# A three-layer graph network with attention: attention in seven stages instead of five, and layer 0's side work spread over more groups

## The chip, the cores and the metric

The kernel runs on one core of a Trainium2 chip. Its time is the device time of one execution in microseconds (us), and less is better. The core has five engines that work side by side, each through its own queue of instructions in a fixed order: TensorE (PE; its weight loads are shown apart as PEld), VectorE (DVE), ScalarE (ACT), GpSimd (POOL) and SyncE (SP), which here only issues transfers. They wait for each other by semaphores. Transfers (DMA) between the main memory and the core's memory are issued by SP, ACT and POOL.

## The reference, cut to what matters

There are 12500 nodes of 256 values and 200000 edges, sorted by their target `dst`. Three layers average over the edges; then one attention step follows, with four heads of 16 values.

```python
# layers 0, 1, 2 (relu after the first two)
agg  = segment_sum(x[src], dst, N)
x    = x @ W_self + (agg * inv_deg[:, None]) @ W_neigh + b
...
# attention
ZU   = einsum('nd,kdr->knr', Z, U)
zs, zd = ZU[:, src, :], ZU[:, dst, :]
logits = (zs * zd).sum(-1) / 4
alpha  = softmax of logits over the edges of one target
agg    = segment_sum(alpha[..., None] * zs, dst)
ssa    = einsum('k,knr,kdr->nd', w, agg, U)
Z_half = 0.5 * Z + 0.5 * ssa
grad   = Z_half + 0.5 * (Z_half - Z_half @ Dmat.T @ Dmat) @ Dmat
x = layernorm(Z + relu(grad - 0.05))
```

## The kernel before, in words

**Groups.** Because edges are sorted by target, 1792 successive edges (14 tiles of 128) touch a range of at most 128 targets. There are 112 such groups. The sum over the edges of a group is a product with a one-hot matrix (`oh`, L453: edge against target), 14 tiles added up in one PSUM bank. What a group's first target still had from the group before it is added by one more product (`carry`, L460). The sources' rows come by indirect transfers that POOL issues, one for each tile of 128 edges, so 14 a group (`gather`, L119).

**Sage layers.** Layers 1 and 2 do this for the targets of lower number (76 groups), and layer 0 for 94 groups. The other targets are handled densely: first a table of counts (how many edges lead from a source to a target) is formed by products of two one-hot matrices (`form`, L603 to L638: DVE makes `oa` and `ob` at L622, PE multiplies at L630, ACT turns the result to bytes at L633), and then the table multiplies all source rows (`sweeps`, L673 to L755, the product at L740). For that, x is split into two parts that add up to it (`split_x`, L499 to L529), and the position where each target's edges end is counted (`row_ends`, L532 to L541; `count_ends`, L554). In layer 0 all of this runs beside the groups. How much of it goes with which group is planned by hand: `due(l, g)` says how many steps of the sweeps are to be done by group g, `built(g)` how many steps of forming, and the loop at L893 to L917 hands them out between the stages of the groups, with ten splits of x a group. GA, G1 and GB are the groups where these plans bend.

**Attention.** `fast_attention` (L929 to L1029) is a generator for each group. A `yield` ends a stage, and the loop at L1019 to L1028 takes each living group on by one stage in a round. In the first stage, group g loads `zn`, `zb`, `zT` and the row for `ohT` by SP, starts 14 gathers of `zs` by POOL, makes `oh` (DVE) and `ohT` (ACT, L958 and L959), splits `zn` in two (`z2`), multiplies (`pD`, L970: the target's values for each edge, in two halves of seven tiles), and forms from it the logits (DVE `zz` L977, `lg` L980), their exponentials (ACT L983) and a copy of these in PSUM (ACT L985), the weighted rows (DVE `wf` L986, the last to read `zs` and `pD`), and their two parts (`w`, ACT L989 and DVE L990). The second stage sums over the edges (`pA`, L993 and L460). The third reads the sums (ACT `part` L1000, DVE `acc` L1002), divides (`den`, `ag`, L384 to L387) and transposes (PE `pT` L1006). The fourth makes the gradient step (ACT `agT` L394, PE `pO` L376 and L377). The fifth ends it (ACT `g` L401, DVE L402 and the layernorm L332 to L337) and stores by SP.

**What sets the order.** A tile has as many buffers as its `bufs` says; the next user of a buffer waits for the last reader of the one before it. `zs` has six, and `pD` two, one for each half.[...] On PE the order is that of the source, since `in_order` chains every group of products to the one before it. On DVE, ACT, POOL and SP the order is fixed when the program is built, from the order of the source and from what is expected to be ready. It isn't always that of the source: the trace shows L401 of an older group between L983 and L985 of a newer one.

Of the kernel before, what the change touches and what calls it, by code (L numbers as in the profile page):

```python
# [9 lines left out]
F32 = mybir.dt.float32  # L10
F32R = mybir.dt.float32r
# [11 lines left out]
P = 128  # L23
NB = 125
TE = 125
GT = 14
# [11 lines left out]
ZB = 2  # L38
# [9 lines left out]
def tile_gnn_resnorm(  # L48
# [16 lines left out]
    K, _, R = u.shape  # L65
    KR = K * R
    DC = D // P
    NBLK = N // NB
    NG = -(-E // GE)
    L = len(w_self)  # L70
    AW = KR + K
    N0 = N - ND * P
    NQ = -(-N // P)
# [3 lines left out]
    NU = ND // SG0  # L77
    U0 = NU - NDL[0] // SG0
    parts = [*range(U0, NU), *range(U0)]

    def part_at(u):

        return max(0, (E * (N0 + u * SG0 * P) // N - SLACK) // GE - GD)
# [4 lines left out]
    needs = [part_groups[u] - part_at(U0) if u >= U0 else NM - part_at(U0) + part_groups[u] for u in range(NU)]  # L88
# [78 lines left out]
    rel = const.tile([P, NG, GT], F32, name="rel")  # L167
# [18 lines left out]
    with tc.tile_pool(name="prep", bufs=1) as prep, \  # L186
# [42 lines left out]
        for nd, c in cuts.items():  # L229
            a, m = c.GS, c.NGS - c.GS  # L230
# [28 lines left out]
        for i, c in enumerate(cuts.values()):  # L259
            a = NM + 2 + 2 * i  # L260
# [176 lines left out]
    def after(first, then):  # L437

        tc.add_manual_dep(then.ins, first.ins.name, AFTER, reason="the order of the work")
# [4 lines left out]
    def group_consts(cps, n=P):  # L444

        c = cps.tile([P, n], F32, name="gconst")
        nc.vector.tensor_copy(c, iota[:, :n])
        return c

    def onehot(wk, nodes, r, dt=F32, name="oh", op=OP.is_equal, bufs=2):  # L450

        oh = wk.tile([P, GT, P], dt, name=name, bufs=bufs)
        nc.vector.tensor_tensor(oh, r.unsqueeze(2).to_broadcast([P, GT, P]),  # L453
                                nodes.unsqueeze(1).to_broadcast([P, GT, P]), op=op)
        return oh
# [6 lines left out]
    def fast_sage():  # L462
        with ExitStack() as fx:
            wp = fx.enter_context(tc.tile_pool(name="sage_w", bufs=1))
            wk = fx.enter_context(tc.tile_pool(name="sage", bufs=2))
# [12 lines left out]
            nodes = group_consts(cps)  # L478
# [73 lines left out]
            counted = [0]  # L552

            def count_ends(pool, n):  # L554
                for g in ends_of[counted[0]:n]:
                    row_ends(pool, g)
                    counted[0] += 1
# [199 lines left out]

            PER = SG0 * P // NC
            BUILDS = 3 + NU * PER
            GA, G1, GB = 3, 7, 62  # L760

            def due(l, g):
                sg, ahead = (SG, 0) if l else (SG0, G1)
                n, end = NDL[l] // sg * NQ, cuts[NDL[l]].NGS - LAG - sg // 2
                if g >= end:
                    return n + (2, 2, 4)[l] * min(sg, 2 * (g + 1 - end))
                if l:
                    return n * (g + 1) // end

                return max(0, n * (g + 1 - G1) // (GB - G1) // 2 if g < GB else n - n * (end - g - 1) // (end - GB) // 2)  # L770

            def built(g):
                if g < GA:
                    return g + 1
                if g < G1:
                    return 3 + PER * (g + 1 - GA) // (G1 - GA)
                return min(BUILDS, 3 + PER + (BUILDS - PER - 3) * (g + 1 - G1) // (GB - G1))

            turn = 0
            for l in range(L):  # L780
# [6 lines left out]
                with ExitStack() as lx:  # L787
# [5 lines left out]
                    if l == 0:  # L793
                        tk = lx.enter_context(tc.tile_pool(name="tabs", bufs=1))
# [4 lines left out]
                    def group(g):  # L799
# [10 lines left out]
                        oh = onehot(wk, nodes, srel, F32R if halved else F32)  # L810
# [58 lines left out]
                            nc.scalar.activation(part, pa[:, D:], AF.Copy)  # L869
                            nc.vector.tensor_add(before[:, :D], part, pa[:, :D])  # L870
                        sums = before[:, :D] if l else pa[:, :D]
                        if l == 0 and g == 0:
                            count_ends(tk, needs[U0])
                        mean = wk.tile([P, D], F32, name="mean", bufs=3)
                        nc.scalar.activation(mean, sums, AF.Copy, scale=inv[:, g:g + 1])  # L875
                        if not l:
# [15 lines left out]
                    live, stages = [], (2, 2, 4)[l]  # L892
                    for g in range(cut.NGS + stages // 2):  # L893
                        units, turns = [], [s for s in live for _ in range(2)]
                        if g < cut.NGS:
                            live.append(group(g))
                            todo, more = due(l, g) - done, built(g) - formed if l == 0 else 0
                            done, formed = done + todo, formed + more
                            n = max(todo, more)
                            for i in range(n):  # L900
                                units += [forming] * ((i + 1) * more // n - i * more // n)
                                units += [steps_] * ((i + 1) * todo // n - i * todo // n)
                            next(live[-1])
                        if l == 0 and g < cut.NGS:

                            soon = min(NU, 1 + max(0, built(g + 1) - 3 + PER - 1) // PER)
                            count_ends(tk, max(counted[0] + 1, max(needs[u] for u in parts[:soon])))
                            for _ in range(10):
                                next(xsplit, None)
                        n = len(turns) + 1  # L910
                        for i in range(n):
                            for u in units[len(units) * i // n:len(units) * (i + 1) // n]:
                                next(u, None)
                            if i < len(turns):
                                next(turns[i])
                        if g >= stages // 2:
                            live.pop(0)  # L917
# [11 lines left out]
    def fast_attention():  # L929
        loads[0] = None  # L930
        H = GT // 2
        with tc.tile_pool(name="att", bufs=2) as wk, \
                tc.tile_pool(name="att_c", bufs=1, space=PSUM) as cps, \
                tc.tile_pool(name="att_ps", bufs=1, space=PSUM) as ps:
            nodes = group_consts(cps)
            order, sums = [None], [None]

            def in_order(first, last):
                if order[0] is not None:
                    after(order[0], first)  # L940
                order[0] = last

            def group(g):

                zb = wk.tile([P, D], F32, name="zb", bufs=8)
                zT = wk.tile([P, DC, P], F32, name="zT", bufs=6)
                zn = wk.tile([P, KR], F32, name="zn", bufs=3)
                load_rows([(zn, zu_d), (zb, z_d), (zT, zt_d)], g)

# [4 lines left out]
                zs = wk.tile([P, GT, KR], F32, name="zs", bufs=6)  # L954
                for j in range(GT):
                    gather(zs[:, j], zu_d, srcI[:, g, j:j + 1])
                oh = onehot(wk, nodes, rel[:, g], F32R, bufs=3)
                nc.scalar.activation(ohT.rearrange("p j e -> p (j e)"), rT, AF.Abs, bias=npidx)  # L958
                nc.scalar.activation(ohT.rearrange("p j e -> p (j e)"), rT, AF.Relu, scale=-1.0, bias=1.0)  # L959

# [2 lines left out]
                nc.scalar.activation(z2[:, :, 0], zk, AF.Copy)  # L963
                nc.vector.tensor_tensor(z2[:, :, 1], zk, z2.bitcast(F32)[:, :, 0], op=OP.subtract)

                w = wk.tile([P, GT, 2 * AW], F32R, name="w", bufs=3)
                for a in (0, H):

                    pd = ps.tile([P, (H + 1) * 2 * KR], F32, name="pD", bufs=2)
                    mm = [nc.tensor.matmul(pd[:, j * 2 * KR:(j + 1) * 2 * KR], ohT[:, a + j],  # L970
                                           z2.rearrange("p k i r -> p (k i r)"), start=True, stop=True)
                          for j in range(H)]
                    in_order(mm[0], mm[-1])

                    zg = zs[:, a:a + H].rearrange("p t (k r) -> p (t k) r", r=R)
                    zz = wk.tile([P, H * K, 2, R], F32, name="zz")
                    nc.vector.tensor_mul(zz, zg.unsqueeze(2).to_broadcast([P, H * K, 2, R]),  # L977
                                         pd[:, :H * 2 * KR].rearrange("p (m i r) -> p m i r", i=2, r=R))
                    lg = wk.tile([P, H, K], F32, name="lg")
                    nc.vector.reduce_sum(lg.rearrange("p t k -> p (t k)"), zz.rearrange("p m i r -> p m (i r)"),  # L980
                                         axis=AX.X)
                    wf = wk.tile([P, H, AW], F32, name="wf")
                    nc.scalar.activation(wf[:, :, KR:], lg, AF.Exp, scale=0.25)  # L983
                    pe = pd[:, H * 2 * KR:H * (2 * KR + K)].rearrange("p (t k) -> p t k", k=K)
                    nc.scalar.activation(pe, wf[:, :, KR:], AF.Copy)  # L985
                    nc.vector.tensor_mul(wf[:, :, :KR].rearrange("p t (k r) -> p t k r", r=R),  # L986
                                         zs[:, a:a + H].rearrange("p t (k r) -> p t k r", r=R),
                                         pe.unsqueeze(3).to_broadcast([P, H, K, R]))
                    nc.scalar.activation(w[:, a:a + H, :AW], wf, AF.Copy)  # L989
                    nc.vector.tensor_tensor(w[:, a:a + H, AW:], wf, w.bitcast(F32)[:, a:a + H, :AW], op=OP.subtract)  # L990
                yield
                pa = ps.tile([P, 2 * AW], F32, name="pA")
# [22 lines left out]
                yield  # L1015

            live = []  # L1019
            for g in range(NG + 4):  # L1020
                if g < NG:
                    live.append(group(g))
                    next(live[-1])
                old = live[:-1] if g < NG else live
                for s in old:
                    next(s)
                if g >= 4:
                    live.pop(0)  # L1028
            assert not live  # L1029

# [203 lines left out]
```

## Time and profile before

| | |
|---|---|
| median of 3 runs | 8820.85 us (8773.32 to 8844.72) |
| the profiled execution | 8849.94 us, its span 8848.1 us |
| granted clock of PE, mean | 0.744 |
| PE busy | 5720.5 us (65%) |
| PE weight loads | 4442.3 us (50%) |
| DVE busy | 3939.4 us (45%) |
| ACT busy | 3599.7 us (41%) |
| POOL busy | 4894.3 us (55%) |

The profile names a group of instructions by its line and the tile that it writes and reads (`pD<-z,ohT`), with a count (x14). "Idle before" is the time that the engine did nothing just ahead of an instruction, and behind the arrow stands what ended it; "issue" and "remote" are waits whose end the profile can't name. The ends of PE's products are modelled. PE's sequence of stages can be told by the lines: layer 0 has L844, layers 1 and 2 have L838, attention has L970.

The chain of work that ended last gives every line a small share:

```profile
PE 9%; issue 7%; another core or an unknown queue 6%; DVE 5%; POOL 2%; ACT 2%; DMA 1%; DVEq 0%; ACTq 0%
```

Its shares add up to 32% of the span, so it covers attention and little before it, and some two fifths of it carry no name of an engine's work (issue, and a queue that the profile can't name).

### The profile page before, as it was taken

How to read it: one execution, taken by the hardware profiler on the slowest of the kernel's cores; microseconds unless marked ns; L12 is line 12 of the kernel's file. 1: busy time of each engine (PE TensorE's matmuls, PEld its weight loads, DVE VectorE, ACT ScalarE, POOL GpSimd, SP SyncE). 2: the span in 40 equal slices, each digit the busy share in tenths (PEclk: the TensorE clock that was granted, in tenths of full speed). 3: DMA queues.
4: the chain of work that ended last, by engine and by line, in shares of the span. 5: the costliest groups of instructions: out<-in, count | busy, mean ns of one | idle time of the engine just before them, and what ended most of it. 6: DMA issues, size and time to landing. Idle time of an engine off the chain costs nothing. (4 is left out here: it accounts for less than half of the span.)

```text
span 8848.1 us, 86603 instructions
## 1 busy us (share of the span) xinstructions
PE 5720.5 (65%) x23308; PEld 4442.3 (50%) x23308; DVE 3939.4 (45%) x10013; ACT 3599.7 (41%) x6544; POOL 4894.3 (55%) x5038
## 2 busy tenths in 40 slices
PE   4666676777757777777677787877524444444445
PEld 2344454555546656666456665666423333333334
DVE  4544444433433333334434444444524544544455
ACT  2433443434434444444344443444324444444444
POOL 4444555555546655555555554555366666666653
PEclk7787888878778888888788898898755555555555
DMA  6644555566646666666466665666322322322232
GB/s 186 218 157 157 161 177 166 176 202 207 204 153 195 201 195 191 205 202 198 156 182 189 181 197 171 189 186 185 106 62 82 86 84 84 87 85 84 83 86 67
DMA packets 878809, 1367.35 MB, mean 155 GB/s; under 512 B 191091, under 2 KB 533131, under 8 KB 874208
## 3 DMA queue, kind: packets, MB, share of 16 engines
q1 hardware_dynamic: 629744, 802.71, 28.3%
q0 software_dynamic: 216000, 504.16, 20.4%
q10 hardware_dynamic: 32559, 54.81, 1.8%
q8 instruction: 187, 3.06, 0.1%
q14 instruction: 319, 2.61, 0.1%
HBM read 1150.87 MB, written 210.33 MB: 154 GB/s over the span
## 5 line engine op out<-in xcount | busy, mean ns | idle before, releaser
L119 POOL DMA_INDIRECT xg<-h_d,srcI x2128 | 2111.5, 992 | 1698.0 <-issue 479.3
L740 PE MATMUL px<-c,hz 128*128 128x512 f32 x7840 | 2500.3, 457 | 378.6 <-issue 254.7
L740 PEld LDWEIGHTS px<-c,hz 128*128 128x128 f32 x7840 | 1616.5, 212 | 1103.5 <-issue 649.7
L119 POOL DMA_INDIRECT zs<-zu_d,srcI x1568 | 1490.4, 951 | 993.8 <-issue 440.1
L119 POOL DMA_INDIRECT xg<-in_x_dram,srcI x1274 | 1230.9, 966 | 1150.1 <-PE pA L844 571.3
L734 ACT ACTIVATE c<-c 128x1024 fp32r<-128x1024 uint8 (+1 forms) x1176 | 1067.1, 911 | 1477.0 <-remote 648.4
L453 DVE TENSOR_TENSOR oh<-rel,gconst 128x1792 fp32r<-128x1792 f32 (+1 forms) x358 | 722.7, 2019 | 1539.2 <-remote 861.0
L1006 PE MATMUL pT<-ident,ag 128*64 128x128 f32 x112 | 47.1, 421 | 1330.0 <-DVE ag L387 1207.2
L833 DVE TENSOR_TENSOR hl<-xg,hl 128x256 fp32r<-128x256 f32 x2128 | 769.8, 416 | 116.5 <-ACT mean L875 47.6
L831 ACT ACTIVATE hl<-xg 128x512 fp32r<-128x512 f32 x1064 | 613.1, 620 | 500.8 <-remote 135.6
L633 ACT ACTIVATE win<-pc 128x392 uint8<-128x392 f32 x1024 | 478.4, 499 | 693.8 <-remote 311.6
L1006 PEld LDWEIGHTS pT<-ident,ag 128*64 128x64 f32 x112 | 14.4, 128 | 1413.3 <-DVE ag L387 1284.8
L630 PE MATMUL pc<-ob,oa 128*128 128x392 bf16 x1024 | 375.1, 393 | 469.7 <-ACT win L633 287.2
L838 PE MATMUL pA<-hl,oh 128*128 128x512 f32 x2128 | 554.3, 408 | 73.6 <-issue 63.1
L838 PEld LDWEIGHTS pA<-hl,oh 128*128 128x128 f32 x2128 | 410.6, 194 | 179.6 <-issue 71.9
L844 PE MATMUL pA<-xg,oh 128*128 128x258 f32 x1764 | 449.5, 395 | 3.2 <-DVE oh L453 3.0
L352 PE MATMUL pO<-ws,hT 128*128 128x256 f32 x984 | 312.9, 448 | 189.6 <-DVE hT L363 103.9
L986 DVE TENSOR_TENSOR wf<-zs,pD 128x448 f32<-128x448 f32 x224 | 129.9, 617 | 619.5 <-issue 444.5
L970 PE MATMUL pD<-z,ohT 128*128 128x128 f32 x1568 | 362.0, 418 | 59.7 <-issue 24.0
L844 PEld LDWEIGHTS pA<-xg,oh 128*128 128x128 f32 x1764 | 346.8, 199 | 89.6 <-issue 33.5
L977 DVE TENSOR_TENSOR zz<-zs,pD 128x896 f32<-128x896 f32 x224 | 242.6, 1083 | 325.8 <-remote 148.2
L970 PEld LDWEIGHTS pD<-z,ohT 128*128 128x128 f32 x1568 | 348.0, 333 | 60.6 <-issue 41.3
(251 smaller groups left out, 8354.5 us busy)
## 6 DMA issues: line engine op xcount, KB each, us to landing
hz<-hs_d SPq DMA_DIRECT2D x588, 512.0 KB
c<-cnt_d SPq DMA_DIRECT2D x112, 896.0 KB
ohT<-rel_d SPq DMA_DIRECT2D x112, 896.0 KB
hs_d<-hs SPq DMA_DIRECT2D x218, 256.0 KB
cnt_d<-win ACTq DMA_DIRECT2D x32, 1568.0 KB
xg<-h_d,srcI POOLq DMA_INDIRECT x2128
c<-cnt_d SPq DMA_DIRECT2D x56, 448.0 KB
zs<-zu_d,srcI POOLq DMA_INDIRECT x1568
```

What stands on the lines that cost most here:

```text
L119: return nc.gpsimd.indirect_dma_start(out=dst_ap, out_offset=None, in_=table, in_offset=bass.IndirectOffsetOnAxis(ap=idx, axis=0))
L352: mm = [nc.tensor.matmul(po, hT[:, i], wts[i // DC][:, i % DC], start=i == 0, stop=i == 2 * DC - 1) for i in range(2 * DC)]
L453: nc.vector.tensor_tensor(oh, r.unsqueeze(2).to_broadcast([P, GT, P]), nodes.unsqueeze(1).to_broadcast([P, GT, P]), op=op)
L630: mm = nc.tensor.matmul(pc.rearrange("p b d -> p (b d)"), oa[:, c], ob[:, c], start=True, stop=True)
L633: nc.scalar.activation(win[:, :, d:d + NC], pc, AF.Copy)
L734: nc.scalar.activation(c32.rearrange("p (k d) -> p k d", d=P), c8[:, :, b % CB], AF.Copy)
L740: made.append(nc.tensor.matmul(px[f][i], hz[:, b % ZB, a:a + P].bitcast(F32R), c32[:, i * 512:(i + 1) * 512], start=b == 0 and part == 0, ...
L831: nc.scalar.activation(hi[:, j:j + 2, :W], xg[:, j:j + 2, :W], AF.Copy)
L833: nc.vector.tensor_tensor(lo[:, j, :D], xg[:, j, :D], hf[:, j, :D], op=OP.subtract)
L838: mm.append(nc.tensor.matmul(pa, oh[:, j], hl[:, j].rearrange("p i d -> p (i d)"), start=first, stop=stop))
L844: mm.append(nc.tensor.matmul(pa[:, :W], oh[:, j], xg[:, j, :W], start=first, stop=stop))
L970: mm = [nc.tensor.matmul(pd[:, j * 2 * KR:(j + 1) * 2 * KR], ohT[:, a + j], z2.rearrange("p k i r -> p (k i r)"), start=True, stop=True) f ...
```

## The change

In attention a group now goes through seven stages. The loads and the gathers are a stage by themselves. The second stage makes `oh`, `ohT`, `z2` and both halves of `pD`. The third reads `pD` and makes the weights: first the logits, exponentials and their copy for both halves, then the weighted rows and first parts of both, then the second parts of both. The other four stages stay as they were. A round first begins the newest group and then takes on the others from the oldest to the youngest. That was so before as well, but what the newest group began with was everything up to `w`, and now it is its loads and gathers alone. `zT` has seven buffers for six, and `oh` four for three.

In layer 0 the plan is flatter at the start. The first seven counts of ends no longer stand together in group 0; three go with group 0, four with group 1. Forming begins in group 2 for group 0, and its first 128 products are spread over groups 5 to 13, where they stood in groups 3 to 6. x is split in five steps a group for ten. The sweeps begin with group 14 for 7, and two fifths of them are done by group 62, where it was half.

```diff
-            GA, G1, GB = 3, 7, 62
+            GA, G1, GB = 5, 14, 62
...
-                return max(0, n * (g + 1 - G1) // (GB - G1) // 2 if g < GB else n - n * (end - g - 1) // (end - GB) // 2)
+                n1 = n * 2 // 5
+                return max(0, n1 * (g + 1 - G1) // (GB - G1) if g < GB else n - (n - n1) * (end - g - 1) // (end - GB))
 
             def built(g):
                 if g < GA:
-                    return g + 1
+                    return max(0, g + 4 - GA)
...
-                        if l == 0 and g == 0:
-                            count_ends(tk, needs[U0])
...
-                            soon = min(NU, 1 + max(0, built(g + 1) - 3 + PER - 1) // PER)
-                            count_ends(tk, max(counted[0] + 1, max(needs[u] for u in parts[:soon])))
-                            for _ in range(10):
+                            soon = min(NU, 1 + max(0, built(g + 1) - 3 + PER - 1) // PER) if built(g + 1) else 0
+                            count_ends(tk, max(counted[0] + (1 if soon else needs[U0] // 2),
+                                               max((needs[u] for u in parts[:soon]), default=0)))
+                            for _ in range(-(-NQ // ZB // (G1 - 2))):
                                 next(xsplit, None)
...
-                zT = wk.tile([P, DC, P], F32, name="zT", bufs=6)
+                zT = wk.tile([P, DC, P], F32, name="zT", bufs=7)
...
-                oh = onehot(wk, nodes, rel[:, g], F32R, bufs=3)
+                yield
+                oh = onehot(wk, nodes, rel[:, g], F32R, bufs=4)
...
-                w = wk.tile([P, GT, 2 * AW], F32R, name="w", bufs=3)
+                halves = []
                 for a in (0, H):
-
                     pd = ps.tile([P, (H + 1) * 2 * KR], F32, name="pD", bufs=2)
...
                     in_order(mm[0], mm[-1])
+                    halves.append((a, pd))
+                yield
+
+                w = wk.tile([P, GT, 2 * AW], F32R, name="w", bufs=3)
+                weights = []
+                for a, pd in halves:
...
                     nc.scalar.activation(pe, wf[:, :, KR:], AF.Copy)
+                    weights.append((a, wf, pe))
+                for a, wf, pe in weights:
                     nc.vector.tensor_mul(wf[:, :, :KR].rearrange("p t (k r) -> p t k r", r=R),
...
                     nc.scalar.activation(w[:, a:a + H, :AW], wf, AF.Copy)
+                for a, wf, pe in weights:
                     nc.vector.tensor_tensor(w[:, a:a + H, AW:], wf, w.bitcast(F32)[:, a:a + H, :AW], op=OP.subtract)
...
-            live = []
-            for g in range(NG + 4):
+            live, stages = [], 7
+            for g in range(NG + stages - 1):
+                old = list(live)
                 if g < NG:
                     live.append(group(g))
                     next(live[-1])
-                old = live[:-1] if g < NG else live
                 for s in old:
                     next(s)
-                if g >= 4:
+                if g >= stages - 1:
                     live.pop(0)
```

## The prediction

> **What bounds the kernel now.** I read the busy time by stage first. The stages are layer 0 (to 2512 us), layer 1, layer 2 and attention (6360 to 8848). Columns: stretch, length, busy time of PE, its weight loads, DVE, ACT, POOL, granted clock, DMA share, GB/s.
>
> ```profile
> 80.50:195.80 115.30, 51.01 (x283) 40.37 (x282) 52.91 (x92) 28.02 (x59) 45.81 (x49) 0.64 0.62 201
> 195.80:353.10 157.30, 98.59 (x375) 55.74 (x374) 104.64 (x348) 92.96 (x210) 51.69 (x49) 0.71 0.73 247
> 353.10:549.10 196.00, 131.20 (x600) 93.29 (x599) 87.23 (x304) 74.08 (x166) 101.78 (x106) 0.81 0.50 160
> 549.10:1823.70 1274.60, 892.39 (x3778) 633.91 (x3777) 569.50 (x2055) 521.02 (x1177) 656.74 (x682) 0.82 0.52 168
> 1823.70:2511.60 687.90, 506.55 (x2191) 391.13 (x2192) 282.68 (x711) 274.34 (x567) 380.75 (x395) 0.80 0.63 198
> ...
> 6549.30:8744.30 2195.00, 987.63 (x3774) 829.15 (x3774) 1072.03 (x2041) 904.84 (x1530) 1357.24 (x1429) 0.50 0.30 84
> 8762.30:8800.70 38.40, 29.03 (x112) 24.38 (x113) 31.79 (x62) 26.90 (x46) 0.00 (x0) 0.50 0.20 70
> ```
>
> The cuts in layer 0 are the starts of groups 0, 3, 7, 14, 62 and 93 (the mean L875 of each), so a group takes 38.4, 39.3, 28.0, 26.6 and 22.2 us. The sixth row is attention in full run: 1429 gathers are 102 groups of 14, so a round takes 21.5 us, and no engine is busy for two thirds of it. The last row is the end, after the last gather: three rounds in 38.4 us, 12.8 each, with the same instructions less the gathers. So the gathers cost more than their own time. The timeline of one round shows how:
>
> ```profile
> 7606.81 3.23 PE L970 MATMUL pD<-z,ohT 128*128 128x128 f32 x14
> ...
> 7611.78 1.22 PE L377 MATMUL pO<-gu,agT 64*128 64x256 f32 x2
> ...
> 7618.90 0.95 POOL L119 DMA_INDIRECT zs<-zu_d,srcI  x1 [0.30 <-issue]
> ...
> 7622.56 0.47 ACT L401 ACTIVATE g<-pO,shrink 128x256 f32<-128x256 f32 x1 [6.86 <-remote]
> ...
> 7623.15 1.15 DVE L986 TENSOR_TENSOR wf<-zs,pD 128x448 f32<-128x448 f32 x2 [6.90 <-ACT pD L985]
> ...
> 7624.57 0.95 POOL L119 DMA_INDIRECT zs<-zu_d,srcI  x1 [4.73 <-DVE den L385]
> ```
>
> and the same pair of lines at the end, without gathers:
>
> ```profile
> 8783.35 1.22 PE L377 MATMUL pO<-gu,agT 64*128 64x256 f32 x2
> ...
> 8784.61 0.47 ACT L401 ACTIVATE g<-pO,shrink 128x256 f32<-128x256 f32 x1 [1.17 <-PE pO L377]
> ```
>
> At the end L401 starts 1.3 us after L377; in full run 10.8 us after it, and 2.7 us after POOL's last gather is over (7619.85). So what PE has finished is seen late while gathers are sent out one after another, and soon once they pause. L401 stands ahead of the copy L985 on ACT, L985 feeds the product wf (L986), wf frees the buffer of zs, and that lets POOL go on. Start to start a gather takes 1.25 us, 14 take 17.5; the pause takes the other 4.0 of the 21.5. Behind wf on DVE stands ag (L387), and PE's transpose L1006, its sums L993 and the next L970 wait for it. The list of waits from 6600 to 8800 (total us, times, longest) agrees:
>
> ```profile
> PE pT L1006 <- DVE ag L387: 1151.7, 98, 23.5
> ACT g L401 <- remote: 446.7, 66, 8.3
> ...
> POOL zs L119 <- DVE den L385: 407.3, 90, 12.6
> ```
>
> **What the Trainium skill says.** "Perfetto Trace Analysis", section "Tensor Engine Instruction (MATMUL, LD_WEIGHTS)": a matmul's shown end is estimated, and its acknowledgement and semaphore lie outside the shown window. The trace agrees (L377 shown over at 7613.0, its reader released at 7622.5), which is why I time PE by its readers. "DMA: Bandwidth & Descriptors", section "Anatomy of one DMA — SWDGE (gpsimd) path": about 2 us fixed per transfer, mostly the receipt. That fits the 2.7 us from the last gather to the release; no page says that such transfers hold back PE's results. "SBUF — State Buffer", "Who interferes with whom": DVE can lock GpSimd out. Not here: a gather takes 941 to 947 ns in the minimum and median. "TensorE: Matmul & The Clock Gate", "What's actually happening": the clock is halved by default. Attention has 0.50 throughout, in both states above.
>
> **The change, part by part.**
>
> *Attention, work.* No instruction is added or removed. Per round DVE has 242.6+241.4+226.2+145.3+129.9 us over 112 groups = 8.8 us in its five large rows, about 11.7 with the small ones; ACT some 9.5. Neither binds against 17.5.
>
> *Attention, order on PE.* Its order is written out by hand. Before: L970 of group g, L376/377 of g-3, L1006 of g-2, L993 of g-1. After, in round r: L376/377 of r-5, L1006 of r-4, L993 of r-3, L970 of r-1. With h = r-1 the cycle reads h, h-3, h-2, h-1 from L970 on: the same cycle. "A round behind" therefore moves DVE and ACT against PE, not PE. Cost of the order itself: 0.
>
> *Attention, DVE and ACT.* Oldest first puts acc, den and ag ahead of zz, so L1006 and L993 need not wait for wf; only L970 does (its two PSUM buffers are freed there). When POOL goes on, PE then has L970 and L376/377 ahead of it (3.2 + 2.0 + 1.2 = 6.4 us) where it now has 0.9 + 3.2 + 0.6 + 6.4 us. What PE ends in the first 5 us after the restart is seen at once (L1000, which reads L993 and L460, starts at 7629.84, 5.3 us after it and straight behind ACT's work before), later work late. So in the next round zz and wf should often be done before POOL has sent its 14 gathers: no pause after that round. But then nothing lets PE's results through either. The trace has this case: two rounds start at 7235.6 and 7249.2, 13.7 us apart, POOL runs on to 7269.9, and the next transpose comes at 7283.3. Together 47.7 us, 23.8 a round, with 12.5 us of pause. And at the start POOL sends 112 gathers in 140 us without a pause, while PE issues 3 sets of L970 and 1 of L993.
>
> So a round takes 17.5 + S/k, with one pause S in k rounds. Now k = 1, S = 4.0. After: k = 2, and S is 2.7 to 4.7 us until results are seen (say 3.7), then zz and lg of both halves 2(1.083+1.078) = 4.3, exp and its copy 0.4, wf 1.2, and acc, den, ag and g ahead of them 1.2: 10.8. That gives 17.5 + 5.4 = 22.9, **1.4 more than now, over 103 rounds +145 us**.
>
> *Buffers, loads, halves.* zT 7 and oh 4 only follow the longer life of the tiles: 0. The four loads and 14 gathers stand alone in a first stage, before the older stages' store on SP; SP issues five transfers of 0.3 to 0.7 us a round, and POOL nothing else: 0, hidden under 17.5 us, and if SP were late it would be ohT, used a round later. Holding back the split of w until both halves are weighted delays L989 of the first half by about 2 us; behind it on ACT stands the next ohT, and L993 reads w a round later: 0. Two more rounds of filling cost nothing that the gathers, six zs buffers ahead, don't cover; uncovered, two end rounds, 25 us.
>
> *Layer 0.* The counts of ends (8 in group 0, 2.0 us of DVE and 14 matmuls each), the splits of x (10 a group in groups 0 to 4) and the first 128 count products (32 a group in groups 3 to 6) are spread: 3 to 4 counts, 5 splits over ten groups, 14 products a group in groups 5 to 13, no sweep steps before group 14. Now groups 0 to 13 take 468.6 us. In groups 3 to 6 DVE is busy 104.6 of 157.3 us; halving its load there and taking 3.5 steps away from groups 7 to 13 should leave 25 us a group (they take 28.0 with 16 products and 3.5 steps, and 22.2 is what groups without products take): 350, **-119**. Groups 14 to 61 get 18.7 products for 16.3 and 3.25 steps for 3.56. A product costs 0.58 us of DVE, 0.39 of PE, 0.50 of ACT; its price in group time lies between 0 (groups wait for gathers anyway) and 0.7 (38.1 - 27 us for 16 more, groups 5 and 6 against later ones). I take 0.5: 2.33 x 0.5 - 0.31 x 1 = 0.9 a group, **+43**. Groups 62 to 90 get 8.1 steps for 6.8, 1.8 us of PE each, of which PE has 6 us a group to spare: 0 to 2.4, I take 0.8, **+25**. Layer 0 together -50, bounds -120 and +40. Layers 1 and 2 aren't touched: 0.
>
> *Sum.* +145 - 50 = +95 us on the profiled execution of 8849.9. That one is 29 us above the median of 8820.85, so I put the difference on the median: **8916**, slower by 1.1%. About 1% (88 us) is what a measurement can tell from no change.
>
> **Rivals.** *Nothing moves in attention* (0.25): L401 keeps its place ahead of L985, its product L377 is still seen only in the pause, k stays 1. For it: PE's cycle is the same. Only layer 0 counts: 8770. *Faster* (0.20): late results still trickle through, as L376 does now (L377 is the one that waits for the pause), so that when POOL pauses only the last half of zz and wf is left, S = 6.6, 20.8 a round, -75; with the better end of layer 0 -195: 8630. It decides from S below 8.0 at k = 2. Against it: in the case above DVE's next reader of PE waits 22 us (7252.6 to 7274.6) and nothing trickles through. *Much slower* (0.10): the new order on ACT or DVE puts a late reader ahead of zz, so that one round needs two pauses: 25 us a round, +360: 9130. *The change doesn't do what it says* is the second half of the first rival.
>
> **Chances and range.** The forecast (0.45, own range 8830 to 9020) is slower by over 1% in somewhat over half of its cases; with the rivals: faster 0.22, within 1% 0.33, slower 0.45. For 8 in 10: 8640 (the faster rival) to 9080 (the pairs at their measured 23.8 a round, +237, and layer 0 at +20).
>
> **What would show it.** Right: runs of 28 or more gathers without a pause, pauses of about 11 us, half as many of them, L1006 no longer waiting for ag; layer 0's groups 0 to 13 near 350 us. Wrong: one pause per 14 gathers as now (first rival), or pauses under 8 us for every two rounds (second).

## The result, and the profile after

The changed kernel takes 8907.08 us (median of 4 runs, 8900.54 to 8916.93) where the kernel before, now with 4 runs, takes 8797.08 us. The ratio is 1.0122, with a 95% interval of 1.009 to 1.0153: slower by 1.2%. The forecast was 8916 us. It stood for +95 us on the median of 8820.85 known then; measured are +110 us on 8797.08, so the closeness of the two totals is in part luck.

The profiled executions differ by less, 8898.7 against 8848.1 us of span, because the one of before (8849.94 us with what lies around its span) was 53 us slower than the median. Their 50.6 us divide well: from the mean of group 0 to that of group 93 layer 0 is 53.1 us shorter (2378.0 for 2431.1), attention from its first gather to the end is 114.5 us longer (2597.7 for 2483.2), and the rest, the end of layer 0 and layers 1 and 2, is 10.8 us shorter.

**Layer 0.** The stretches are again those from group 0, 3, 7, 14 and 62 to the next, with the last ending at group 93; columns as in the same view of before.

```profile
81.00:173.90 92.90, 45.59 (x238) 36.27 (x238) 41.43 (x68) 23.46 (x50) 37.47 (x40) 0.67 0.62 198
173.90:295.10 121.20, 58.41 (x266) 43.06 (x267) 54.53 (x146) 38.98 (x84) 56.25 (x59) 0.70 0.61 198
295.10:501.90 206.80, 115.55 (x490) 79.18 (x490) 91.75 (x286) 69.55 (x158) 91.40 (x98) 0.74 0.53 173
501.90:1764.00 1262.10, 903.36 (x3864) 629.44 (x3860) 622.98 (x2295) 563.76 (x1271) 668.03 (x690) 0.83 0.53 170
1764.00:2459.10 695.10, 534.25 (x2367) 420.35 (x2368) 287.90 (x715) 299.08 (x615) 383.06 (x395) 0.83 0.68 216
```

Groups 0 to 6 went from 38.4 and 39.3 to 31.0 and 30.3 us each, groups 7 to 13 from 28.0 to 29.5, groups 14 to 61 from 26.6 to 26.3, and groups 62 to 92 from 22.2 to 22.4. In the second row DVE is busy 54.5 of 121.2 us, where it was 104.6 of 157.3, and yet a group takes 30 us: no engine is busy for half of the stretch.

**Attention.** The list of waits from 6600 to 8800 (total us, times, longest), the same stretch as before:

```profile
DVE zz L983 <- remote: 638.2, 69, 12.7
...
PE pT L1015 <- DVE ag L387: 541.3, 42, 26.3
...
PE pD L970 <- DVE wf L994: 463.4, 61, 13.9
ACT g L401 <- remote: 435.6, 22, 25.0
...
POOL zs L119 <- DVE wf L994: 386.5, 38, 14.6
```

The transpose (L1006 before, L1015 now) waits for `ag` half as long as it did (1151.7 us), and two waits have come in its place: PE's `pD` waits for `wf`, and DVE's `zz` waits 638 us for something that the profile can't name (the last section tells what). It was 81.7 us before:

```profile
DVE zz L977 <- remote: 81.7, 18, 7.2
```

L401 waits as long in sum, but 22 times for 66, and up to 25 us for 8. Counted from POOL's rows, 102 runs of gathers with pauses of 4.5 us in the mean have become 63 with 9.2 us: one of 112 gathers at the start as before, then 40 of 28, 21 of 14 and one of 42. The timeline of one pause:

```profile
7689.42 1.22 PE L377 MATMUL pO<-gu,agT 64*128 64x256 f32 x2
...
7698.08 1.09 DVE L983 TENSOR_TENSOR zz<-zs,pD 128x896 f32<-128x896 f32 x1 [5.63 <-remote]
...
7709.72 0.95 POOL L119 DMA_INDIRECT zs<-zu_d,srcI  x1 [0.30 <-issue]
...
7711.37 1.09 DVE L983 TENSOR_TENSOR zz<-zs,pD 128x896 f32<-128x896 f32 x1 [10.63 <-remote]
...
7714.96 0.47 ACT L401 ACTIVATE g<-pO,shrink 128x256 f32<-128x256 f32 x1 [23.59 <-remote]
...
7716.08 0.42 PE L1015 MATMUL pT<-ident,ag 128*64 128x128 f32 x1 [25.44 <-DVE ag L387]
...
7718.91 0.62 DVE L994 TENSOR_TENSOR wf<-zs,pD 128x448 f32<-128x448 f32 x1 [1.21 <-ACT pD L991]
...
7721.64 1.12 POOL L119 DMA_INDIRECT zs<-zu_d,srcI  x1 [10.97 <-DVE wf L994]
```

POOL sends 28 gathers, from 7675.5 on. L377 is shown as over at 7690.64, but its reader L401 starts at 7714.96, 4.3 us after the last gather. The semaphore events kept with the trace tell where the time lies: the update of PE's semaphore that releases L401 comes at 7714.93, 24.3 us after that shown end and 0.03 us ahead of L401. So the signal itself comes late, and not ACT's answer to it. Between the two readings of `pD` DVE stands still for 10.6 us. Only in the pause does the chain from L401 over `lg` and the copy L991 to `wf` run off, and POOL goes on after 10.97 us. The pauses come in a fixed turn, mostly 28 gathers and 11 to 15 us, 28 and 6 to 8, 14 and 5 to 6: five rounds, over and over.

That turn is in the program itself. This is DVE's order of instructions in a round (by the tile written; the layernorm left out), as built:

```
before, every round   g w ag z2 w oh zz acc lg zz den sh lg wf wf den
after, five rounds    g lg wf wf sh oh w w zz acc lg den zz den
in turn               g ag lg z2 z2 wf wf w acc sh den oh w den zz ag lg zz
                      g lg oh wf wf acc w w den zz den lg ag zz sh lg wf wf
                      g w z2 z2 sh oh w acc den zz den zz ag lg lg
                      g z2 z2 oh wf wf acc den sh den ag zz w w lg zz
```

Before, each `ag` stood behind both `wf`. Now each `ag` stands ahead of the two `wf` that follow it (the first line has no `ag`, the second has two), but where exactly `zz` and `wf` fall goes through five cases.

### The profile page after: what moved, and what is told of

Read it like the earlier page. It is cut to its first block, busy times and chain, and to the rows that moved or that the text cites. A ratio compares the mean times of both kernels' runs of the same rounds, so it can differ in the third digit from the quotient of the medians.

```text
span 8898.7 us, 86986 instructions
## 1 busy us (share of the span) xinstructions
PE 5713.4 (64%) x23308; PEld 4449.7 (50%) x23308; DVE 3924.7 (44%) x10013; ACT 3601.3 (40%) x6544; POOL 4908.7 (55%) x5038
## 5 line engine op out<-in xcount | busy, mean ns | idle before, releaser
L740 PE MATMUL px<-c,hz 128*128 128x512 f32 x7840 | 2455.0, 453 | 353.1 <-issue 218.5
L453 DVE TENSOR_TENSOR oh<-rel,gconst 128x1792 fp32r<-128x1792 f32 (+1 forms) x358 | 721.4, 2015 | 1655.9 <-remote 1001.9
L970 PE MATMUL pD<-z,ohT 128*128 128x128 f32 x1568 | 366.3, 418 | 600.1 <-DVE wf L994 483.8
L970 PEld LDWEIGHTS pD<-z,ohT 128*128 128x128 f32 x1568 | 345.8, 330 | 617.5 <-issue 574.6
L1015 PE MATMUL pT<-ident,ag 128*64 128x128 f32 x112 | 47.2, 421 | 876.7 <-DVE ag L387 626.8
L1015 PEld LDWEIGHTS pT<-ident,ag 128*64 128x64 f32 x112 | 14.4, 128 | 956.9 <-DVE ag L387 664.7
L1002 PE MATMUL pA<-w,oh 128*128 128x136 f32 x1568 | 362.1, 418 | 0.0
```

What stands on the lines that cost most here:

```text
L740: made.append(nc.tensor.matmul(px[f][i], hz[:, b % ZB, a:a + P].bitcast(F32R), c32[:, i * 512:(i + 1) * 512], start=b == 0 and part == 0, ...
L1002: mm = [nc.tensor.matmul(pa, oh[:, j], w[:, j], start=j == 0, stop=g == 0 and j == GT - 1) for j in range(GT)]
```

## The experiments

### The two parts by themselves

In the first kernel only the changes of layer 0 are made, in the second only those of attention, each exactly as in the diff.

> Attention is as before; layer 0 is as after. Theory (the two parts are separate, layer 0 gains what its groups show in the traces, 53 us): 0.994 of before, the POOL runs in attention of 14 gathers with a pause of 4 to 5 us. Rival (layer 0's gain is only seen because something later is shifted, or the trace's 53 us is scatter): 0.999 to 1.001.

> Layer 0 is as before; attention is as after. Theory: attention alone loses what the changed kernel shows from its first gather to its end, 2597.7 against 2483.2 us, so +115 us or 1.013 of before, with runs of 28 and 14 gathers. Rival (the new attention is no slower, the loss lies where the stages meet): within 0.3% of before.

Layer 0 alone gives 0.9966 (0.9949 to 0.9983), attention alone 1.0141 (1.0108 to 1.0173). On 8797 us that is -30 and +124, together +94, beside +107 for both at once, so within their intervals the parts add up. Attention is as theory had it: 41 runs of 28 and 22 of 14 gathers. Layer 0 gains less than the two traces had shown, 30 us where their difference was 53. Three traces with the new layer 0 (after, this one, and e3 below) give 2378.0, 2412.1 and 2384.5 us from group 0 to 93, the two with the old one 2431.1 and 2422.5; so the 53 us of one pair is the largest difference that these five give, and 10.4 us the smallest. (The nine other kernels below, all with the new layer 0 and most of them measured on other chips, lie between 2358.2 and 2403.5 us.)

### Only the order of the stages

```diff
+                first = max(0, g - stages + 1)
+                if 0 <= g - 2 < NG:
+                    s = old.pop(g - 2 - first)
+                    old.insert(0, s)
                 for s in old:
                     next(s)
```

> As after (seven stages, both halves' products together, zT 7, oh 4, layer 0 new), but in each round the stage with zz and wf is written out first, ahead of the older groups. Theory (only the order of DVE and ACT costs): the rounds of attention are 21.5 us again with one pause of 4 to 5 us per 14 gathers, and the whole is layer 0's gain away from before: 0.994. Rival (the extra stage, the held-back split of w or the buffers cost): runs of 28 stay, 1.007 or more.

It gives 0.9987 (0.997 to 1.0004). The seven stages, the halves, the buffers and layer 0 are those of after, and DVE's and ACT's programs come out in the order of before, one round like the next. The pauses are those of before, too: 98 runs of 14 gathers, 4.7 us of pause in the mean, 21.6 us a round, and the old pair of waits:

```profile
PE pT L1015 <- DVE ag L387: 1056.9, 89, 23.6
ACT g L401 <- remote: 518.3, 79, 8.2
```

So the loss of attention is nearly all one of order. The value is above the forecast 0.994, as e1's is, and it is also above e1's: the medians are 8866.43 and 8848.03 us, of 22 runs each on the same chip, 18 us or 0.2% apart, little more than their scatter (8822 to 8904 us) lets one tell. In the traces the stretch from the first gather to the end is 15 us longer (2493.9 for 2478.7). The added stage, the held-back split of `w` and the buffers together can have cost about that much; which of them did was not tested.

### Without the gathers

> As after, but in attention the 14 gathers of a group are left out; one plain load on SP's queue brings as many rows of zu_d (the first 1792, so the sums are not the reference's). Theory (the gathers sent by POOL hold back what PE has finished; nothing else in the loop takes more than 12.8 us a round): rounds of 12.5 to 14 us, attention some 1450 us, 7.7 to 7.8 ms in all. Rival (the order of DVE and ACT itself is slow, or the moved bytes are): rounds of 18 us or more, above 8.3 ms.

One run took 7567.91 us. From 6400.7 to 7554.4 there are 111 rounds of 10.4 us, less than the forecast 12.5 to 14 and less than half of after's 22.8, with twice the bytes per us (the last two columns are DMA share and GB/s; after has 0.28 and 80):

```profile
6500.00:7500.00 1000.00, 930.02 (x3543) 780.21 (x3542) 968.94 (x1921) 833.00 (x1438) 0.00 (x0) 0.50 0.60 174
```

and one round's end on its timeline:

```profile
7004.71 1.22 PE L377 MATMUL pO<-gu,agT 64*128 64x256 f32 x2
...
7005.97 0.48 ACT L401 ACTIVATE g<-pO,shrink 128x256 f32<-128x256 f32 x1 [2.24 <-PE pO L377]
```

L401 starts 1.3 us after L377 starts, 0.04 us after its shown end, and DVE is busy 97% of the time. What holds PE's results back is neither PE's order nor the moved bytes: it goes with POOL's gathers. Whether their issue by POOL does it or the transfers that they start is not separated, here or below.

### A break of POOL's own

```diff
                 for j in range(GT):
-                    gather(zs[:, j], zu_d, srcI[:, g, j:j + 1])
+                    i = gather(zs[:, j], zu_d, srcI[:, g, j:j + 1])
+                    after(sent[0], i) if sent[0] is not None else None
+                    sent[0] = i
+                    for _ in range(6 if j == 13 else 0):
+                        i = nc.gpsimd.iota(idle, pattern=[[1, 512]], base=0, channel_multiplier=0,
+                                           allow_small_or_imprecise_dtypes=True)
+                        after(sent[0], i)
+                        sent[0] = i
```

Dependences keep POOL's instructions in this order. Nothing reads `idle`. On DVE and ACT the order is that of the kernel without the break.

> Layer 0 new, attention as before (that is e1), but POOL writes six small iotas of 128x512 into a spare tile behind the 14 gathers of each group, about 3.3 us if one takes the 0.55 us that the fp16 one of the start takes; the order on every engine stays. Theory (results of PE come through about 2.7 us after the last gather, whatever makes POOL stop): the break takes the place of the pause, rounds of 17.5 + 3.3 = 20.8 us where e1 has 21.5, about 0.99 of before and 0.992 of e1. Rival (the pause is time that DVE and ACT need for zs, and not bound to POOL's silence): the break is added or hidden in part, 21.5 to 24.8 us a round, 1.00 to 1.04.

> After, with the same six iotas behind the 14 gathers of each group; the order on every engine stays as in after. Theory (after's order is slow only because POOL runs on past 14 gathers while PE's results are held back): rounds of about 20.8 to 21.5 us, no runs of 28, 0.985 to 0.995 of before, although POOL does more work. Rival (after's order of DVE and ACT is slow in itself): 22.6 us or more a round, 1.012 or more.

> As e5, but three iotas behind the 7th and three behind the 14th gather: two breaks of about 1.65 us instead of one of 3.3. Theory (nothing comes through before about 2.7 us of silence): the short breaks don't help, POOL's own time is 20.8 us and a pause of some 3 us still comes on top: 23 to 24 us a round, 1.02 to 1.03. Rival (any gap lets results through): 20.8 us, like e5.

e5 gives 0.9889 (0.9873 to 0.9905), e6 0.9897 (0.988 to 0.9915), and e7 8672.91 us in one run, as fast as e5 (8681.19). POOL on e5's timeline:

```profile
7203.18 0.94 POOL L119 DMA_INDIRECT zs<-zu_d,srcI  x1 [0.30 <-issue]
7204.14 3.77 POOL L962 IOTA idle<- 128x512 f32 x6
7208.06 0.96 POOL L119 DMA_INDIRECT zs<-zu_d,srcI  x1 [0.15 <-issue]
```

and all that POOL waits for in the same kernel, from 6400 to 8640 (more than 0.5 us in total):

```profile
POOL zs L119 <- issue: 434.9, 1461, 2.1
POOL zs L119 <- DVE sh L459: 1.1, 7, 0.2
```

The first line is the usual 0.3 us between two gathers. After each 14 gathers POOL is away for 3.9 us, and it no longer waits for `zs` to be freed, in either order: e6 has the 21.35 us a round of e5, where after has 22.76. So after's order is not slow in itself, since it keeps up with 21.35 us a round; it is slow because POOL runs on. ("A round" is here and in the table the mean from the start of the 13th group's gathers to that of the last group's.) Where e5's gain lies was not as expected: a round takes 21.35 us, against 21.44 in e1 and the forecast 20.8. The gain on e1 (0.9889 / 0.9966, some 68 us) is at the end. From the last gather to the end e1 needs 90.9 us and e5 26.1, which is about two rounds of before's end (12.8 us each) where it was seven: nothing has piled up behind POOL. In e6 it is both: 2384.9 us from the first gather to the last for 2523.6, and 26.4 us of end for 74.2.

e7 went against theory: two gaps of 2.0 us let enough through. How short can a gap be? In the table a gap is the measured time from the end of a gather to the start of the next one where POOL does not wait for `zs`; between two gathers of one burst it is 0.30 us.

> As e7, but one iota of 0.56 us behind the 7th and one behind the 14th gather, so two gaps of about 0.85 us where e7 has two of 2.0. Theory (a gap lets results through if it is long enough; e7 shows that 2.0 us twice a round is enough): these are too short, PE's results are held again, POOL is stopped for zs as in e1: 17.5 + 1.1 + some 3 us, 21.5 to 22.5 a round, 0.995 to 1.005. Rival (any instruction of POOL other than a gather lets results through, whatever its length): POOL alone sets the round, 17.5 + 2 x 0.85 - 0.6 = 18.6 to 19.2 us, about 0.965.

> As e9, but the two iotas write 128x16 and take some 0.13 us each. Theory (the length of the gap decides): as without them, runs past 14 and pauses of 3 to 5 us, 21.5 us a round, 0.995 to 1.0. Rival (any other instruction on POOL lets results through): 17.8 to 18.2 us a round, about 0.955.

> As e5, but three iotas behind the 14th gather instead of six: one gap of about 2.0 us a round (e7 has two of them, e5 one of 3.9). Theory (a gap of 2.0 us lets through what PE has finished, and one a round is enough, as the pause of before is one a round): POOL never waits for zs, 17.5 + 2.0 - 0.3 = 19.2 us a round, some 190 us less than e5 over 103 rounds, 0.965 to 0.97 of before. Rival (2.0 us is too short for one gap alone, e7 lives by having two): POOL is still stopped for zs, 21 to 24 us a round, 0.99 to 1.02.

> As e11 and e5, with four iotas behind the 14th gather: one gap of about 2.8 us a round, between the 2.0 that did nothing and the 3.9 that took the pause away. Theory (results come through about 2.7 us after the last gather, as in before): 2.8 us is just enough, POOL never waits for zs, 17.5 + 2.8 - 0.3 = 20.0 us a round, some 110 us less than e5, 0.975 to 0.98 of before. Rival (it takes longer than 2.8 us of silence until DVE and ACT have used what came through): POOL is stopped for zs after the gap in most rounds, 21 us or more a round, 0.99 to 1.00.

| behind gather | gap | ratio to before (95%) | us a round | last gather to the end |
|---|---|---|---|---|
| none (e1) | | 0.9966 (0.9949 to 0.9983) | 21.44 | 90.9 |
| 7 and 14, 128x16 (e10) | 0.33 | 1.0013 (0.9998 to 1.0027) | 21.63 | 95.7 |
| 7 and 14, one iota (e9) | 0.74 | 1.0143 (1.0116 to 1.017) | 23.11 | 87.3 |
| 7 and 14, three (e7) | 2.0 | one run | 21.18 | 26.1 |
| 14, three (e11) | 2.0 | 1.0008 (0.999 to 1.0026) | 21.52 | 90.0 |
| 14, four (e12) | 2.6 | 0.9986 (0.9972 to 0.9999) | 21.65 | 85.0 |
| 14, six (e5) | 3.9 | 0.9889 (0.9873 to 0.9905) | 21.35 | 26.1 |

e9 and e10 exclude that any other instruction of POOL lets results through; it is a matter of how long POOL is silent. In e11 and e12 the rival was right. POOL keeps to 19.3 and 19.9 us a round for the first nine and twelve rounds. Then it is stopped for 12.4 and 11.3 us, and from there on it waits for `zs` in most rounds. This is e11's list from 6400 to 8700:

```profile
POOL zs L119 <- DVE den L385: 245.0, 93, 10.6
```

With the iotas its pauses are mostly 3.3 to 4.9 us long, about as those of before. One reading is that a single silence must hold what comes through and what ACT and DVE do with it, and that 2.6 us is too short for that and 3.9 enough. But the sum of the silences in a round orders these kernels as well: 1.5, 2.0 and 2.6 us (e9, e11, e12) were not enough, 3.9 and 4.0 us (e5, e7) were. No run separates the two readings. e9 came out slower than either theory had it: 51 runs of 28 gathers, with pauses of 8.8 to 11.4 us, the pattern of after in before's order. Why so short a gap brings that about was not settled.

### One wait taken away

In the kernel of e1, L401 is put behind both copies of the weights (L985) on ACT, so that `wf` no longer stands behind the late product L377 (`late` is the newest group's second L985):

```diff
-        nc.scalar.activation(g, pg, AF.Relu, bias=shrink[:n])
+        relu = nc.scalar.activation(g, pg, AF.Relu, bias=shrink[:n])
+        if late is not None:
+            after(late, relu)
```

> Layer 0 new, attention as before, but on ACT the activation of g (L401) is put behind both copies of the weights (L985) by a dependence, so that wf no longer waits for the held back product L377. Theory (one pause in k rounds): POOL isn't stopped after 14 gathers, runs of 28 and more come, each pause grows to 10 us or more: 22 to 24 us a round, 1.00 to 1.03 of before. Rival (L401's wait is simply gone): 18 to 19 us a round, 0.96 to 0.97.

It gives 1.0237 (1.0216 to 1.0257), 2.7% slower than e1 (1.0237 / 0.9966). There are 48 runs of 28 gathers with pauses of 12.0 to 12.6 us, and 23.8 us a round. The timeline around one pause:

```profile
7053.29 0.94 POOL L119 DMA_INDIRECT zs<-zu_d,srcI  x1 [0.31 <-issue]
...
7058.95 2.02 DVE L455 TENSOR_TENSOR oh<-rel,gconst 128x1792 fp32r<-128x1792 f32 x1 [16.78 <-remote]
...
7065.28 1.23 DVE L988 TENSOR_TENSOR wf<-zs,pD 128x448 f32<-128x448 f32 x2
...
7066.77 0.94 POOL L119 DMA_INDIRECT zs<-zu_d,srcI  x1 [12.54 <-DVE wf L988]
```

As the forecast had said of the change, `wf` is ready early and POOL runs on past 14. DVE stands for 16.8 us ahead of `oh` (L453 in before), from the middle of the run until 4.7 us after its last gather, and two groups' work is left for one longer pause. But the edit did more than take a wait away. L401 is also the last to read `pO`, and L376 of the next group now waits for that. From 6600 to 8800:

```profile
PE pO L376 <- ACT g L401: 944.6, 46, 22.5
```

In before this wait was 0.2 us in all of attention. On DVE `den` and `ag` also come out a few places later. So e8 shows that 28 gathers in a row with one long pause are slow, in another order than after's; it doesn't show that the wait taken away is what made it so, and not the new one.

## Why the prediction was right, point by point

**PE's results are seen late while gathers follow each other.** Right, in attention. It is shown by e4 (10.4 us a round without gathers), by e5 and e6 (a break of POOL alone cures both orders), and by e9 and e10 (a short one does not).

**PE's order is the same cycle, cost 0.** Right: as built, each round on PE is L1015, 14 of L1002, L460, 14 of L970, L376, L377, the same as before with its own line numbers.

**One pause in two rounds, T = 17.5 + S/k = 22.9.** Right in kind and nearly in size. After the first 112 gathers there are 104 groups and 62 pauses, k = 1.68 for 2. From start to start the gaps hold 628.4 us, 10.1 each, less the usual 1.25, so S = 8.9 for 10.8. Together that is 17.5 + 8.9/1.68 = 22.8, and the trace has 22.76 a round. Both terms were some 20% too high and made up for each other, which is luck. That the built order would go through five cases, a third of the runs staying at 14, was not foreseen. e8, where 48 of the 56 runs behind the start have 28 gathers, comes closest to k = 2: by the same reckoning k = 1.86 and S = 11.5, so 17.5 + 11.5/1.86 = 23.7, measured 23.8. From first gather to last it is +127.5 us in after. The end behind it was 12.9 us shorter, which the forecast had at 0 or +25: hence +114.5 for the forecast +145.

**Only `pD` will wait for `wf`, and the transpose no longer for `ag`.** Half right. In the page PE's idle time ahead of `pD` rose from 59.7 to 600.1 us, and 483.8 of it end with `wf`; ahead of the transpose, what ends with `ag` fell from 1207.2 to 626.8. It doesn't go away, because `ag` itself is held behind a `zz` or a `g` that waits for PE.

**Stages, halves and buffers at nothing.** Nearly right: e3 leaves about 18 us for them, its distance from e1.

**Layer 0, -50.** The sum fits the traces' -53 by luck, and e1's timed -30 less well; its terms are not right. The forecast had -119 for groups 0 to 13, +43 for 14 to 61 and +25 for 62 to 92; the traces show -48, -13 and +7. The term of groups 0 to 13 took DVE's load for the time of a group. In groups 3 to 6 DVE's 104.6 us fell by half and a group still takes 30 us, with DVE, PE and POOL each busy less than half of the stretch; 25 us was too low a price. What bounds these groups instead was not tested. The products and steps moved to later groups were priced at 0.9 and 0.8 us a group and cost -0.3 and 0.2: the lower bound, 0, would have been the better choice.

**The rivals.** That nothing moves in attention is excluded by e2. The faster case needed S under 8.0 at k = 2. S is 8.9 with k = 1.68, 5.3 us a round where that rival needed less than 4.0. Nowhere does a round need two pauses, so the much slower case did not come.

## What to carry to other kernels

When an engine's reader is released only after another engine's burst of transfers ends, look at how long that burst runs before you reorder anything: here the kernels in which POOL mostly ran past 14 gathers were slower, whether that came from the order of the stages (after), from another dependence (e8) or from two very short breaks (e9), since the silence is what lets the other engines go on. A stop of fixed length after each burst can be better than the wait it replaces, though the engine that stops is the one that bounds the loop: e5 takes 0.989 of before, of which 0.9966 is layer 0's part. It gained at the end and not in the round. And where a builder fixes the order on some engines, compare the built order of two kernels, since a change in the source can turn one repeated round into a cycle of several.

## What was not expected of the hardware

A silence of POOL of 0.74 us twice a round did not help (e9 was even slower), 2.0 us twice was enough, 2.0 or 2.6 us once was not, and 3.9 us once was. Whether the longest silence or their sum decides is open.

The semaphore events of the traces narrow down where PE's results are held. In e4 from 6500 to 7500 us, without gathers, each of the 605 updates of PE's semaphore comes within 0.02 us of a product's shown end. In after from 6487 to 8784 us, 280 of the 538 that were recorded come more than 1 us after the last such end before them, and up to 24.5 us. DVE's and ACT's come within 0.03 us of an end in both. The waits that the profile calls remote are these: in the same stretch of after, all 194 such waits of DVE and ACT of more than 1 us end within 0.03 us of a late update of PE's semaphore. It is so outside attention as well: in layers 1 and 2, where POOL gathers too, 779 of 2063 come more than 1 us late (after, 2600 to 6280).

So the delay lies ahead of the semaphore's update, not between the update and its reader. Whether the product itself ends late, since its shown end is modelled, or only its signal is held, and what in the chip does it, is open.
